# Layer 1's second table made inside the rounds, and the order of the lagging block and of the last groups

## The chip, the cores and the metric

The kernel runs on one core of one Trainium2 chip. A core has five engines with an instruction queue each: TensorE (PE) multiplies matrices into PSUM, VectorE (DVE) and ScalarE (ACT) compute on SBUF and PSUM, GpSimd (POOL) here mostly issues gathers, and SyncE (SP) issues plain transfers. Each engine takes its instructions strictly in order and waits on semaphores where an instruction needs the result of another engine or of a transfer. The metric is the time of one execution on the device, in microseconds (us); the verdict compares medians over several runs.

## The reference

A graph network of two layers over 6250 nodes with 128 features and 106250 edges sorted by their target `dst`. Cut to what matters:

```python
h = relu(layernorm(x))
# layer 0: attention over the edges of each target
xl, xr = h @ Wl + bl, h @ Wr + br
m = leaky_relu(xl[src] + xr[dst] + edge_weight1 @ We, 0.2)
logits = m @ att
ex = exp(logits - segment_max(logits, dst)[dst])
out = segment_sum(xl[src] * ex, dst) / (segment_sum(ex, dst) + 1e-16) + bias_out
h = gelu(h + out)
x = x + batchnorm(h)                 # mean and variance over all nodes
# layer 1: messages
h = relu(layernorm(x))
em = concat([h[src], h[dst]]) @ msg_w + msg_b
em = relu(layernorm(em) * msg_g + msg_beta) * edge_weight
messages = segment_sum(em, dst) / count
gate = sigmoid(h @ gate_w + gate_b)
h_new = relu(layernorm(concat([h, messages]) @ upd_w + upd_b) * upd_g + upd_beta)
x = x + gate * h_new + (1 - gate) * h
```

## The kernel before

**Two arms.** A flag is computed on the chip from `dst`. Where the targets are sorted and every block of 1024 edges touches few enough nodes, the arm `fast()` runs, else `general()`. The conditions are columns of the tile `wide`, four before the change (L282 to L292).

**Tables.** Layer 0 gathers rows of `xl_d` by `src`. Layer 1 uses linearity: `h[src] @ msg_w[:128]` and `h[dst] @ msg_w[128:]` are computed per node into the tables `a_d` (the source ends) and `b_d` (the target ends, "the other ends"). `a_d` is gathered by `src`, so all of it must be written before the first gather. `b_d` is read in windows of 126 consecutive rows, because the targets of one block are consecutive.

**Rounds.** Both layers walk 104 blocks (`NS`) of 1024 edges (8 tiles of 128), one block `s` per round: eight gathers on POOL (`gather`, L200), a window of the target table into `W` (`load`, L878), a product with a one-hot matrix that spreads the window over the edges (`spread`, `expand` L895), DVE and ACT work, and a product with a second one-hot matrix `oh` that sums a block's edges into its window (`agg_ps`, L1110 and L1370). The sums go to `res0_d` or `res1_d` (`flush`, `store` L898).

**The lagging block.** In layer 0 the sums need the maximum of each target, which is found for four blocks at a time (`maxima`, a generator of eight working steps that alternate between DVE and PE). So round `s` also finishes block `u = s - 7`: its one-hot `oh` (L1079), its weights `glw` (L1082, and eight scalings at L1094 on ACT; after the last gather half of them at L1092 on DVE), its product (L1110). After the last gather, eight rounds (`s` = 104 to 111) work off the lag. In layer 1 the lag is one block.

**Groups of nodes.** A group of four node tiles is finished (`nodes` in layer 0, `nodes1` in layer 1, also generators) once every block that can touch it has been stored; `rounds_of` gives the round. The last group (13 groups, the last of two tiles) can only start after the last block: `both` alternates its steps with those of the group before.

**The middle.** Between the layers lie the batch norm (`bn`, L1150 to L1158) and a loop over 13 chunks of 512 nodes: `mix` (DVE), `centre` (PE), `split` (ACT and POOL), a product `var_ps` for the variance, and one product `mm` per tile of 128 nodes (L1203), 257 columns wide: 128 for `a_d`, 128 for `b_d`, one for the gate. ACT scales the `b_d` half and the gate (L1212), DVE the `a_d` half (L1213), SP writes both (L1216, L1217).

**Order.** Inside `tc.manual_schedule()` the order on each engine is that of the program text; semaphores are placed automatically. A tile of a pool with one buffer can be filled again only when all readers of the one before are done. The PSUM pool `ps_1` of layer 1 has one buffer for each of the tags `nt`, `nz`, `agg1_ps` and the constants.

Of the kernel before, what the change touches and what calls it, by code (L numbers as in the profile page):

```python
# [16 lines left out]
P = 128  # L17
# [23 lines left out]
SLACK = 96  # L41
TN = 4
# [11 lines left out]
def kernel(  # L54
# [167 lines left out]
    with tc.tile_pool(name="pre", bufs=2) as pp, tc.tile_pool(name="pre1", bufs=1) as p1, tc.tile_pool(  # L222
# [59 lines left out]
        wide = p1.tile([NS, 4], F32, name="wide")  # L282
# [8 lines left out]
        for k in range(4):  # L291
            V.tensor_add(nbad[:NS, :], nbad[:NS, :], wide[:, k : k + 1])  # L292
# [452 lines left out]
    def fast():  # L745
# [165 lines left out]
        def both(a, b):  # L911

            left = [b, a]
            while left:
                for g in list(left):
                    if next(g, True):
                        left.remove(g)
# [9 lines left out]
        with tc.tile_pool(name="e0", bufs=2) as ep, tc.tile_pool(  # L927
# [61 lines left out]
            def nodes(g):  # L989
# [36 lines left out]
                S.activation(hT_sb[:, ns], hT_sb[:, ns], AF.Gelu)  # L1026
                yield
# [21 lines left out]
            steps, group = None, None  # L1049
# [9 lines left out]
            for s in range(NS + LAG + 1):  # L1059
# [10 lines left out]
                if s < NS:  # L1070
                    ps = pss.pop(s)
                    V.tensor_tensor(ps, ps, gl[:, :, :D], ALU.add)  # L1072
                    S.activation(ps, ps, AF.Relu)  # L1073
                if steps is not None:
                    next(steps, None)
                if 0 <= u < NS:
                    b, q = divmod(u, SB)
                    oh = ep.tile([P, ST, P], F32, name="oh")
                    V.tensor_tensor(oh, over_tiles(iota_ps, ST), over_features(dl_c[:, u, :], ST),  # L1079
                                    ALU.is_equal)  # L1080
                    glw = ep.tile([P, ST, W0], F32, name="glw")
                    V.tensor_copy(glw[:, :, D:], exm[b][:, q])  # L1082
                if s + 2 < NS:
                    one_hot_t(ps_1, "mx", s + 2, 0, *wins[s + 2])
                if u >= 1 and s < NS:
                    flush(u - 1)
                if 0 <= u < NS:
                    glu = gls.pop(u)
                    for j in range(ST):
                        f = exm[b][:, q, j, 1:2]  # L1090
                        if s >= NS and j % 2:
                            V.tensor_scalar(glw[:, j, :D], glu[:, j, :D], f, None, op0=ALU.mult)  # L1092
                        else:
                            S.activation(glw[:, j, :D], glu[:, j, :D], AF.Copy, scale=f)  # L1094
                if s >= NS:
                    flush(u - 1)
                if s < NS:
# [13 lines left out]
                if s < NS and s % SB == SB - 1:  # L1111
                    steps = maxima(s // SB)
                    next(steps, None)
                elif steps is not None:
                    next(steps, None)
# [14 lines left out]
            both(group, nodes(NGR - 1))  # L1130
# [9 lines left out]
        wm = fs.tile([P, 2 * D + 1], F32, name="wm")  # L1140
        V.tensor_copy(wm[:, : 2 * D], w1[:, : 2 * D])
        V.tensor_copy(wm[:, 2 * D :], w1[:, 3 * D : NW1])
        with tc.tile_pool(name="md", bufs=2) as mp, tc.tile_pool(
# [44 lines left out]
            for c in range(NC):  # L1188
# [11 lines left out]
                for j in range(n):  # L1200
                    t = c * TN + j
                    mm = ps_t.tile([P, 2 * D + 1], F32, name="mm")
                    T.matmul(mm, hT_sb[:, t * P : (t + 1) * P], wm, start=True, stop=True)  # L1203
                    outs.append(mm)
# [4 lines left out]
                tab = mp.tile([P, TN, 2 * D + 1], F32, name="tab")  # L1209
                for j, mm in enumerate(outs):  # L1210
                    r = rstd_c[:, c * TN + j : c * TN + j + 1]
                    S.activation(tab[:, j, D:], mm[:, D:], AF.Copy, scale=r)  # L1212
                    V.scalar_tensor_tensor(tab[:, j, :D], mm[:, :D], r, b1[:, :D], op0=ALU.mult, op1=ALU.add)  # L1213
                V.tensor_copy(gate[:, ts], tab[:, :n, 2 * D])
                rows_ = slice(c * CH, c * CH + n * P)
                nc.sync.dma_start(a_d[rows_].rearrange("(t p) f -> p t f", p=P), tab[:, :n, :D])  # L1216
                nc.sync.dma_start(b_d[rows_].rearrange("(t p) f -> p t f", p=P), tab[:, :n, D : 2 * D])  # L1217
# [7 lines left out]
        with tc.tile_pool(name="e1g", bufs=6) as gp, tc.tile_pool(name="e1", bufs=2) as ep, tc.tile_pool(  # L1225
# [22 lines left out]
            def nodes1(g):  # L1248
# [7 lines left out]
                yield  # L1256
# [11 lines left out]
                yield  # L1268
                mT = e1.tile([P, m, P], F32, name="mT", tag="mT" + z_)
                z = e1.tile([P, m, D], F32, name="z", tag="z" + z_)  # L1270
                tp = ps_1.tile([P, TN, P], F32, name="nt")
                for j in range(n):
                    T.transpose(tp[:, j, :], fin[:, 0, j, :D], ident)
                S.copy(mT[:, :n, :], tp[:, :n, :])
                yield
                zp = ps_1.tile([P, TN, D], F32, name="nz")
                for j in range(n):
                    T.matmul(zp[:, j, :], mT[:, j, :], u2, start=True, stop=False)
                    T.matmul(zp[:, j, :], h_sb[:, t0 + j, :], w1[:, 2 * D : 3 * D], start=False, stop=True)
                for j in range(n):  # L1280
                    V.scalar_tensor_tensor(z[:, j, :], zp[:, j, :], rstd_c[:, t0 + j : t0 + j + 1],
                                           b1[:, 2 * D : 3 * D], op0=ALU.mult, op1=ALU.add)
                yield
# [19 lines left out]
                tp = ps_1.tile([P, TN, P], F32, name="nt")  # L1303
                xp = ps_1.tile([P, TN, P], F32, name="nz")
                for j in range(n):
                    T.transpose(tp[:, j, :], h_sb[:, t0 + j, :], ident)
                    T.transpose(xp[:, j, :], x_sb[:, t0 + j, :], ident)
                for j in range(n):
                    V.scalar_tensor_tensor(z[:, j, :], tp[:, j, :], keep[:, t0 + j : t0 + j + 1], z[:, j, :],
                                           op0=ALU.mult, op1=ALU.add)  # L1310
# [7 lines left out]
            group = None  # L1318
            due = rounds_of(1)
            for s in range(2):  # L1320
# [5 lines left out]
            for s in range(NS + 2):  # L1326
                u = s - 1
                if s + 2 < NS:
# [42 lines left out]
                if s in due:  # L1371
                    finish(group)
                    group = nodes1(due[s])
                if group is not None:
                    next(group, None)
            both(group, nodes1(NGR - 1))
# [49 lines left out]
```

## Time and profile before

| | us |
|---|---|
| three runs | 2317.82, 2320.14, 2320.94 (median 2320.14) |
| the profiled execution, its time | 2316.21 |
| its span (first to last instruction) | 2314.1 |
| first gather of layer 0 starts | 61.2 |
| last gather of layer 0 issued | 1104.4 |
| first gather of layer 1 starts | 1216.7 |
| last gather of layer 1 issued | 2256.4 |

Busy time over the span, of the page's first part: POOL 1611.4 us (70%), DVE 1766.5 (76%), PE 1437.2 (62%), ACT 1273.6 (55%). A line of the timeline gives the start, the duration, the engine, the source line, the operation, the tiles, and in square brackets how long the engine had been idle before and what ended the idle time. A line of the windows view gives the stretch, its length, the busy time and the number of instructions of PE, weight loads, DVE, ACT and POOL, then the granted clock of PE, the share of the DMA engines and GB/s.

### The profile page before, as it was taken

The page shows a single profiled execution, that of the slowest core. Times are in us where ns is not written, and L with a number is a line of the kernel's source. Part 1 is how long each engine was busy: PE and PEld are TensorE (multiplying, and loading weights), DVE is VectorE, ACT ScalarE, POOL GpSimd, SP SyncE. Part 2 cuts the span into 40 slices and gives each one's busy share as a digit, 9 for nine tenths or more (in the row PEclk, how much of TensorE's full clock was granted, in tenths as well). Part 3 has the DMA queues.
Part 4 walks back from the last instruction along what each step waited for, and adds up shares of the span by engine and source line. Part 5 has one row for each costly group of instructions (what it writes and reads, how often), then busy time and mean ns, then how long its engine had stood idle before and what let it go on. Part 6 is the DMA issues. An engine that isn't in the chain of part 4 may idle for free.

```text
span 2314.1 us, 30585 instructions
## 1 busy us (share of the span) xinstructions
PE 1437.2 (62%) x8206; PEld 1245.6 (54%) x8206; DVE 1766.5 (76%) x3795; ACT 1273.6 (55%) x4208; POOL 1611.4 (70%) x1703
## 2 busy tenths in 40 slices
PE   5656666566656666666585666666665666566663
PEld 4545555455555555556464555555555555555553
DVE  5578788788788788777655777797797887788786
ACT  5224344443344344443465776777777777777674
POOL 1777777777777777777037777777777777777770
PEclk9679878887787878887787777888888788888886
DMA  5742343332332332332132222232233233233231
GB/s 149 179 132 68 87 142 107 76 76 67 76 77 67 76 77 67 77 76 66 40 112 61 67 76 75 70 80 78 68 80 80 64 80 81 66 81 79 67 79 28
DMA packets 187647, 188.13 MB, mean 81 GB/s; under 512 B 38256, under 2 KB 154960, under 8 KB 187464
## 3 DMA queue, kind: packets, MB, share of 16 engines
q0 software_dynamic: 53792, 110.57, 19.8%
q1 hardware_dynamic: 130812, 75.25, 11.3%
q8 instruction: 66, 1.08, 0.2%
q10 hardware_dynamic: 2860, 0.27, 0.1%
q14 instruction: 117, 0.96, 0.1%
HBM read 142.91 MB, written 43.04 MB: 80 GB/s over the span
## 4 chain that ended last, share of the span: by engine, by line
POOL 31%; DVE 25%; issue 14%; DMA 12%; PE 10%; ACT 6%; DVEq 0%; POOLq 0%; ACTq 0%; another core or an unknown queue 0%; SPq 0%
POOL gl L200 31%; DMA gl<-xl_d,src_c 8%; DVE y L1354 4%; DMA gl<-a_d,src_c 3%; PE agg_ps L1370 3%; DVE m_ps L1072 3%; DVE y L1338 2%; DVE oh L1349 2%; DVE y L1356 2%; ACT sq L1343 2%; DVE oht L891 2%; ACT y L1357 1%; ACT glw L1360 1%; PE mm L1203 1%; DVE lr L1100 1%
## 5 line engine op out<-in xcount | busy, mean ns | idle before, releaser
L200 POOL DMA_INDIRECT gl<-xl_d,src_c x832 | 790.6, 950 | 298.8 <-issue 230.4
L200 POOL DMA_INDIRECT gl<-a_d,src_c x832 | 787.4, 946 | 261.0 <-issue 226.2
L1370 PEld LDWEIGHTS agg_ps<-glw,oh 128*128 128x128 f32 x1664 | 314.3, 272 | 481.6 <-ACT glw L1360 481.6
L890 PE MATMUL dlp<-dl_b,ident_b 104*128 104x512 bf16 x416 | 179.3, 431 | 607.4 <-DVE oht L891 500.1
L1110 PEld LDWEIGHTS agg_ps<-glw,oh 128*128 128x128 f32 x1664 | 295.8, 267 | 228.6 <-ACT glw L1094 209.8
L1370 PE MATMUL agg_ps<-glw,oh 128*128 128x129 f32 x1664 | 341.1, 382 | 90.7 <-ACT glw L1360 81.3
L891 DVE TENSOR_SCALAR oht<-dlp,iota_p 126x512 f32<-126x512 f32 x416 | 309.7, 744 | 97.9 <-PE dlp L890 97.9
L1343 ACT ACTIVATE sq<-y 128x128 f32<-128x128 f32 x832 | 256.9, 309 | 225.3 <-DVE y L1338 202.4
L1073 ACT ACTIVATE m_ps<-m_ps 128x1024 f32<-128x1024 f32 x104 | 104.9, 1008 | 501.1 <-DVE m_ps L1072 249.3
L1110 PE MATMUL agg_ps<-glw,oh 128*128 128x130 f32 x1664 | 299.1, 355 | 22.6 <-ACT glw L1094 10.5
L895 PE MATMUL m_ps<-W,oht 128*128 128x128 f32 x1664 | 255.5, 317 | 12.1 <-DMA oht<-in_edge_weight_dram 6.2
L1072 DVE TENSOR_TENSOR m_ps<-m_ps,gl 128x1024 f32<-128x1024 f32 x104 | 128.0, 1231 | 173.6 <-DMA gl<-xl_d,src_c 164.5
L1360 ACT ACTIVATE glw<-y,ew_c 128x128 f32<-128x128 f32 x832 | 254.5, 389 | 3.4
L895 PEld LDWEIGHTS m_ps<-W,oht 128*128 128x128 f32 x1664 | 238.5, 229 | 20.8 <-DVE lr L1100 11.0
L1094 ACT ACTIVATE glw<-gl,exm 128x128 f32<-128x128 f32 x804 | 245.9, 393 | 0.1
L895 PEld LDWEIGHTS y_ps<-W,oht 128*128 128x128 f32 x1664 | 223.4, 216 | 8.9 <-issue 7.2
L895 PE MATMUL y_ps<-W,oht 128*128 128x128 f32 x1664 | 227.0, 295 | 0.0
L1354 DVE SCALAR_TENSOR_TENSOR y<-y,rs,cst 128x128 f32<-128x128 f32 x832 | 223.2, 340 | 0.0
L1338 DVE TENSOR_TENSOR y<-y_ps,gl 128x1024 f32<-128x1024 f32 x104 | 125.3, 1205 | 47.4 <-DMA gl<-a_d,src_c 45.7
L1343 ACT ACTIVATION_READ_ACCUMULATOR sq<-y 128x1 f32 x832 | 155.0, 186 | 0.0
L1357 ACT ACTIVATE y<-y 128x1024 f32<-128x1024 f32 x104 | 109.9, 1056 | 44.2 <-DVE y L1356 44.2
L1100 DVE TENSOR_REDUCE lr<-m_ps 128x8 f32<-128x1024 f32 x104 | 127.3, 1224 | 3.6
(255 smaller groups left out, 1769.2 us busy)
## 6 DMA issues: line engine op xcount, KB each, us to landing
gl<-xl_d,src_c POOLq DMA_INDIRECT x832
gl<-a_d,src_c POOLq DMA_INDIRECT x832
res<-agg SPq DMA_DIRECT2D x104, 64.0 KB
res<-agg SPq DMA_DIRECT2D x104, 63.5 KB
W<-xr_d SPq DMA_DIRECT2D x104, 63.0 KB
W<-b_d SPq DMA_DIRECT2D x104, 63.0 KB
res<-zt SPq DMA_DIRECT2D x20, 325.0 KB
res<-zt SPq DMA_DIRECT2D x20, 322.5 KB
```

What stands on the lines that cost most here:

```text
L200: GP.indirect_dma_start(out=dest, out_offset=None, in_=table, in_offset=bass.IndirectOffsetOnAxis(ap=idx, axis=0))
L890: T.matmul(dlp, ident_b[:NS, s : s + 1].to_broadcast([NS, P]), dl_b[:, es], start=True, stop=True)
L891: V.tensor_scalar(oht[:WIN, es], dlp[:WIN, :], iota_p[:WIN, :], None, op0=ALU.is_equal)
L895: T.matmul(ps[:, j, :], oht[:, j * P : (j + 1) * P], w, start=True, stop=True)
L1072: V.tensor_tensor(ps, ps, gl[:, :, :D], ALU.add)
L1094: S.activation(glw[:, j, :D], glu[:, j, :D], AF.Copy, scale=f)
L1110: T.matmul(aggs[u], oh[:, j, :], glw[:, j, :], start=(j == 0), stop=(j == ST - 1))
L1338: V.tensor_tensor(y, pss.pop(s), gl, ALU.add)
L1343: S.activation(sq, y[:, j, :], AF.Square, accum_out=rs[:, j : j + 1])
L1354: V.scalar_tensor_tensor(yu[:, j, :], yu[:, j, :], ru[:, j : j + 1], mg_ps, op0=ALU.mult, op1=ALU.mult)
L1360: S.activation(glw[:, j, :D], yu[:, j, :], AF.Copy, scale=ew_c[:, u, j : j + 1])
L1370: T.matmul(aggs[u], oh[:, j, :], glw[:, j, :], start=(j == 0), stop=(j == ST - 1))
```

## The change

1. A fifth column of `wide`: a block whose first target lies beyond 61 times its number plus 64 sets the flag.
2. In layer 0's round the order of the lagging block changes: `oh`, `glw`, the scalings and the store of block `u` come ahead of the work on block `s`, and a step of `maxima` comes after them (except in every fourth round, where it stays right behind `oh`).
3. `both` becomes `in_turn`: the steps of the last two groups follow a written order. In layer 0's last group one `Sqrt` of a constant is added behind the `Gelu`.
4. In the middle the product shrinks to 129 columns, DVE scales all of it in one instruction per tile, ACT no longer scales anything and takes the copy of the gate column from DVE. The `b_d` rows of the first 512 nodes are made there, behind chunk 1.
5. The other twelve pieces of `b_d` are made in rounds 1, 9, 18, 26, 34, 43, 51, 60, 68, 76, 85 and 93 of layer 1: four products at the end of the round into the PSUM tile `nt`, one DVE multiplication and one transfer at the start of the next.
6. `nodes1` is cut into other steps: all its PSUM tiles share the tag `nz`, a wait of one round behind `fetch` goes, products and their readers lie in different rounds. In the last rounds the group before the last is only fetched in round 103, and the one before that is finished in round 104.

```diff
+LEAD = 61
+AHEAD = 64
...
+        V.tensor_scalar(wide[:, 4:5], iota_p[:NS, :], float(LEAD), float(AHEAD), op0=ALU.mult, op1=ALU.add)
+        V.tensor_tensor(wide[:, 4:5], dst_r[:, 0:1], wide[:, 4:5], ALU.is_gt)
-        for k in range(4):
+        for k in range(5):
...
-        def both(a, b):
-            left = [b, a]
-            while left:
-                for g in list(left):
-                    if next(g, True):
-                        left.remove(g)
+        def in_turn(a, b, order):
+            for c in order:
+                next(a if c == "a" else b, None)
+            finish(a)
+            finish(b)
...
                 S.activation(hT_sb[:, ns], hT_sb[:, ns], AF.Gelu)
+                if last:
+                    S.activation(std_c[:, 0:1], eps, AF.Sqrt)
...
-                if s < NS:
-                    ps = pss.pop(s)
-                    V.tensor_tensor(ps, ps, gl[:, :, :D], ALU.add)
-                    S.activation(ps, ps, AF.Relu)
-                if steps is not None:
-                    next(steps, None)
                 if 0 <= u < NS:
                     b, q = divmod(u, SB)
                     oh = ep.tile([P, ST, P], F32, name="oh")
...
+                    if q == 0:
+                        next(steps, None)
                     glw = ep.tile([P, ST, W0], F32, name="glw")
                     V.tensor_copy(glw[:, :, D:], exm[b][:, q])
-                if s + 2 < NS:
-                    one_hot_t(ps_1, "mx", s + 2, 0, *wins[s + 2])
-                if u >= 1 and s < NS:
-                    flush(u - 1)
-                if 0 <= u < NS:
                     glu = gls.pop(u)
...
-                if s >= NS:
+                if u >= 1:
                     flush(u - 1)
+                if s < NS:
+                    ps = pss.pop(s)
+                    V.tensor_tensor(ps, ps, gl[:, :, :D], ALU.add)
+                    S.activation(ps, ps, AF.Relu)
+                if u < 0 or u % SB:
+                    next(steps, None)
+                if s + 2 < NS:
+                    one_hot_t(ps_1, "mx", s + 2, 0, *wins[s + 2])
...
-            both(group, nodes(NGR - 1))
+            in_turn(group, nodes(NGR - 1), "baabbbabbab")
...
-        wm = fs.tile([P, 2 * D + 1], F32, name="wm")
+        wm = fs.tile([P, D + 1], F32, name="wm")
+        def b_product(ps, g):
+            n = min(TN, NT - g * TN)
+            for j in range(n):
+                t = g * TN + j
+                T.matmul(ps[:, j, :], hT_sb[:, t * P : (t + 1) * P], w1[:, D : 2 * D], start=True, stop=True)
+        def b_rows(pool, ps, g):
+            t0, n = g * TN, min(TN, NT - g * TN)
+            tab = pool.tile([P, TN, D], F32, name="tab_b")
+            V.tensor_tensor(tab[:, :n, :], ps[:, :n, :], over_features(rstd_c[:, t0 : t0 + n], n), ALU.mult)
+            nc.sync.dma_start(b_d[t0 * P : (t0 + n) * P].rearrange("(t p) f -> p t f", p=P), tab[:, :n, :])
...
-                    S.activation(tab[:, j, D:], mm[:, D:], AF.Copy, scale=r)
-                    V.scalar_tensor_tensor(tab[:, j, :D], mm[:, :D], r, b1[:, :D], op0=ALU.mult, op1=ALU.add)
-                V.tensor_copy(gate[:, ts], tab[:, :n, 2 * D])
+                    V.scalar_tensor_tensor(tab[:, j, :], mm, r, b1[:, : D + 1], op0=ALU.mult, op1=ALU.add)
+                S.copy(gate[:, ts], tab[:, :n, D])
...
-                nc.sync.dma_start(b_d[rows_].rearrange("(t p) f -> p t f", p=P), tab[:, :n, D : 2 * D])
+                if c == 1:
+                    bp = ps_t.tile([P, TN, D], F32, name="b_ps", tag="mm")
+                    b_product(bp, 0)
+                    b_rows(mp, bp, 0)
...
                 fetch(fin, res1_d, t0, n)
                 yield
-                yield
...
-                yield
...
-                tp = ps_1.tile([P, TN, P], F32, name="nt")
+                tp = ps_1.tile([P, TN, P], F32, name="nt", tag="nz")
                 for j in range(n):
                     T.transpose(tp[:, j, :], fin[:, 0, j, :D], ident)
+                yield
                 S.copy(mT[:, :n, :], tp[:, :n, :])
-                yield
                 zp = ps_1.tile([P, TN, D], F32, name="nz")
...
+                yield
                 for j in range(n):
...
-                yield
                 mv = small.tile([P, TN, 2], F32, name="mv1")
...
-                tp = ps_1.tile([P, TN, P], F32, name="nt")
-                xp = ps_1.tile([P, TN, P], F32, name="nz")
-                for j in range(n):
-                    T.transpose(tp[:, j, :], h_sb[:, t0 + j, :], ident)
+                hp = ps_1.tile([P, TN, P], F32, name="nh", tag="nz")
+                for j in range(n):
+                    T.transpose(hp[:, j, :], h_sb[:, t0 + j, :], ident)
+                yield
+                for j in range(n):
+                    V.scalar_tensor_tensor(z[:, j, :], hp[:, j, :], keep[:, t0 + j : t0 + j + 1], z[:, j, :],
+                                           op0=ALU.mult, op1=ALU.add)
+                xp = ps_1.tile([P, TN, P], F32, name="nx", tag="nz")
+                for j in range(n):
                     T.transpose(xp[:, j, :], x_sb[:, t0 + j, :], ident)
-                for j in range(n):
-                    V.scalar_tensor_tensor(z[:, j, :], tp[:, j, :], keep[:, t0 + j : t0 + j + 1], z[:, j, :],
-                                           op0=ALU.mult, op1=ALU.add)
+                yield
                 V.tensor_tensor(z[:, :n, :], z[:, :n, :], xp[:, :n, :], ALU.add)
...
+            early = {(CH * g - AHEAD - WIN + 1 - 2 * LEAD) // LEAD - 2: g for g in range(1, NCH)}
...
+                if made is not None:
+                    b_rows(ep, *made)
+                    made = None
...
+                if s in early:
+                    made = ps_1.tile([P, TN, D], F32, name="b_ps1", tag="nt"), early[s]
+                    b_product(*made)
-                if s in due:
+                if s in due and s < NS - 1:
                     finish(group)
                     group = nodes1(due[s])
-                if group is not None:
+                if group is not None and s < NS - 1:
                     next(group, None)
-            both(group, nodes1(NGR - 1))
+                if s == NS - 1:
+                    late, last = nodes1(due[s]), nodes1(NGR - 1)
+                    next(late)
+                if s == NS:
+                    finish(group)
+                    next(late)
+            in_turn(late, last, "baaababababa")
```

## The prediction

> **What bounds the kernel now.** I read first the list of costliest groups:
>
> ```profile
> L200 POOL DMA_INDIRECT gl<-xl_d,src_c x832 | 790.6, 950 | 298.8 <-issue 230.4
> L200 POOL DMA_INDIRECT gl<-a_d,src_c x832 | 787.4, 946 | 261.0 <-issue 226.2
> ```
>
> A gather takes 0.94 us and the next starts 0.30 later: 832 at 1.248 are 1038.3 us. Layer 0 took 1044.1 (61.2 to 1105.3), layer 1 1040.7 (1216.7 to 2257.4). In the rounds nothing but POOL counts; a block takes 8 x 1.248 = 9.98 us there. The gaps without gathers remain: 61.2 us in front, 111.4 between the layers, 56.7 at the end. Next, the windows of two pieces of the middle gap:
>
> ```profile
> 1105.00:1160.00 55.00, 26.80 (x147) 23.30 (x146) 35.31 (x116) 22.80 (x60) 0.33 (x1) 0.75 0.16 35
> 1174.00:1210.00 36.00, 36.00 (x194) 29.50 (x193) 20.79 (x71) 27.52 (x74) 19.88 (x11) 1.00 0.49 148
> ```
>
> In the drain of layer 0 no engine is full (DVE 35 of 55): it waits in a ring. In the chunks of the middle PE is busy all 36 us. Then the timeline, the drain:
>
> ```profile
> 1120.46 0.21 DVE L956 TENSOR_TENSOR_SCAN srow<-kS,tx 1x32 f32<-1x32 bf16 x1 [2.21 <-PE tx L952]
> 1126.10 0.15 DVE L969 COPY cc<-tx 32x2 f32<-32x2 f32 x1 [3.11 <-PE tx L966]
> 1133.23 0.19 DVE L982 TENSOR_TENSOR exm<-tx,fst_c 128x32 f32<-128x32 f32 x1 [2.79 <-PE tx L978]
> 1145.71 2.06 PE L1110 MATMUL agg_ps<-glw,oh 128*128 128x130 f32 x16 [0.40 <-ACT agg L1046]
> 1160.07 1.28 ACT L1151 ACT_TABLE_LOAD   x1 [1.05 <-DVE bmv L1150]
> ```
>
> DVE waits for a `maxima` transpose queued on PE behind `agg_ps`, and the next block's `oh` is behind that wait. One chunk of the middle, and the end:
>
> ```profile
> 1181.15 0.69 ACT L1179 ACTIVATE sq<-ctr,bn 128x512 f32<-128x512 f32 x1 [0.55 <-PE ctr L1173]
> 1181.70 1.98 PE L1203 MATMUL mm<-wm,h_sb 128*128 128x257 f32 x8
> 1182.31 0.26 ACT L1207 ACTIVATE std_c<-var_ps,eps 128x4 f32<-128x4 f32 x1
> 1182.60 0.18 DVE L1208 RECIPROCAL rstd_c<-std_c 128x4 f32<-128x4 f32 x1 [0.89 <-ACT std_c L1207]
> ...
> 2257.00 1.13 DVE L1281 SCALAR_TENSOR_TENSOR z<-nz,rstd_c,b 128x128 f32<-128x128 f32 x4 [7.01 <-PE nz L1279]
> 2276.40 0.69 DVE L1298 TENSOR_TENSOR z<-z,ug_r 128x512 f32<-128x512 f32 x1 [4.78 <-ACT z L1295]
> 2290.06 0.27 ACT L1245 COPY agg<-agg_ps 128x129 f32<-128x129 f32 x1 [1.49 <-PE agg_ps L1370]
> 2294.88 0.16 DVE L1258 TENSOR_TENSOR inv<-fin 128x2 f32<-128x2 f32 x1 [1.44 <-DMA fin<-res]
> ```
>
> At the end DVE waits 7.01 and 4.78 us for steps of `nodes1` that stand in front of the last blocks' work.
>
> **Layer 0's drain (1113.6 to 1147.8).** DVE's waits for transposes are 1.59 (L943), 2.21, 3.11 and 2.79: 9.7 us. After the change `oh` (pitch 1.13), `glw` (0.15) and four scalings (0.86), 2.1 us in all, stand ahead of each step, so PE multiplies while DVE prepares the next block; PE needs 2.0 to 3.8 us a block (L1110) plus 0.2 to 0.4 for transposes, DVE 2.1 plus the step's 0.75 to 1.6. I leave 1.6 us of waits, and the last block's logits come 0.2 earlier (no `oh` between): 8.3 gained, `agg_ps` of block 103 ending at 1139.5. Bounds: 5 (half the waits stay, PE at the slow 3.8) and 9.9.
>
> **Layer 0's last groups (1147.8 to 1161.65).** Both `Exp` now come before both `Gelu`, and the `Sqrt` table loads under the statistics. From the end of the last store's copy (1139.8): store and fetch 4.5 (as 2290.33 to 2294.88), maxima 0.75, the other group's `h_sb` 0.65, scaling 2.0, transposes 0.5, `h_sb` 0.5, `Gelu` 0.45, statistics 1.0, rest of the table load and the root 0.85: 1151.0 against 1161.65, so 2.4 gained beyond the drain (bounds 1 and 4). The rows price a table switch at 1.28 us and the next activation at 1.30 after it. The Trainium skill, "ScalarE: Activation LUTs", section "What ACT_TABLE_LOAD costs", adds a drain of about 1.38 us to each; no row here shows it. By the page two removed switches would save some 2.8 us more.
>
> **The middle.** PE per chunk now: `ctr` 0.86, `var_ps` 0.79, `mm` 1.84, sum 3.49, the period. With 129 columns the nearest row is 128 columns at 0.117 per instruction (`m_ps` L895, 16 in 1.87): 8 are 0.94, sum 2.59. But ACT's copy of the gate waits for DVE's last scaling, and the next chunk's `sq` is queued behind it on ACT. Ring: `sq` 0.58, `h_sb` 0.57, root 0.29, reciprocal 0.21, four scalings from PSUM 1.13 (L1281, four), hand-over 0.05, copy 0.1 (as L984 to L1046): 2.95. So this ring takes PE's place. Ten periods: (3.49 - 2.95) x 10 = 5.4, the last being 2.84 now, less 0.6. `b_ps` behind chunk 1 waits for a `mm` buffer and pushes `ctr` of chunk 3: -0.9. In chunk 0 PE is slow (3.77 for `mm`), half of it goes, 2.0 of it seen by `sq` of chunk 2. Behind the last `sq`: 3.55 to the last `a_d` write instead of 4.47: 0.9. Total 6.8. The removed 13 ACT groups of scalings and `b_d` writes lie inside this. SP's loads of `W` now wait for the first `b_d` piece in front of an `a_d` write; SP needs 0.36 a chunk, covered, up to 2 us for one chunk otherwise. Bounds: ring at 3.35 (copy and hand-overs at the 0.26 of L1207 and 0.2): 2.8; PE alone (2.59): 10. A rule against it: the Trainium skill, "VectorE: DVE Perf Modes", section "The TRN2 errata", gives SBUF sources a fixed 224 cycles on ScalarE but 58 on VectorE. By it a copy of four elements is an estimated 0.19 us on ACT, the ring 3.04, and the gain 0.9 less; rows of 0.14 to 0.16 (DVE, L1214) and 0.19 (ACT, L984) agree on the ACT side.
>
> **`b_d` in the rounds.** Twelve times 0.94 on PE, 0.74 on DVE (512 wide, as L1168), a write and SP's next `W` load behind it, about 5 us, needed a round later. DVE stands at the round's start for a product queued behind `agg_ps`: that ended 2.2 us after the next `y` began (1710.80, 1713.00), so 3.2 + 0.7 = 3.9 us late, and `y`, `sq` and all behind them with it. Cover: a round of layer 1 needs 7.53 us (`y` at 1703.27, 1710.80) against 9.98, 20.6 us over 8.4 rounds; a group takes 9.5 of DVE, and its waits of 7.0 and 1.4 go by the new cuts. 14.4 of 20.6, with six gather buffers behind. Cost 0; without the cover 12 x 3.9 = 47.
>
> **The end.** `y` of block 103 ran at 2265.6, its gather landed at 2259.8. With the 7.01 gone and no group work in round 103, it runs at 2260.0. Round 103: 5.6 of DVE, then ACT `y` and `glw` 3.5, `agg_ps` to 2270.6; the copy, block 103's `y`, `glw` and product take 5.2 more: 2275.8 against 2290.03. Some is given back: DVE's last sum of group 10 waits for transposes behind that product (2277.5), and its output write stands on SP ahead of the last store, so store and fetch land at 2282.8, not 2280.5. Group 11 scales from 2277.5 to 2280.2, transposes and copy to 2281.2, product 2283.3, scaling and statistics 2285.5, `z` 2287.6. Group 12 scales 2286.3 to 2288.5; then both share the one buffer `nz`: copy 2289.2, transposes 2290.5, group 11's use 2291.2, group 12's product 2293.1, statistics 2294.7, `z` 2297.0, three weights 2298.4, use 2299.0, transposes 2300.0, sum 2300.5. Before: 2309.84. Gain 9.3; bounds 3.5 (`y` 103 as late as before) and 11.
>
> **The rest at nothing.** The fifth condition's DVE work, 0.12 + 0.15 + 0.13 (L289, L290, L292), lies under DVE's idle 1.0 to 1.5 per `tl` group; 0.4 without. On these inputs every block's first target is at least 61 rows inside the new bound. Layer 0's rounds: the relu on ACT stands behind eight `glw` (2.44), which no longer wait for the gather and are done before it lands.
>
> **Sum.** 8.3 + 2.4 + 6.8 + 9.3 = 26.8: span 2287.3, execution 2316.21 - 26.8 = 2289.4. The median shown was 3.9 above that execution, so 2293.3; I say 2294.
>
> **Rivals.** *Half of it* (chance 0.14): the middle's ring at 3.35 and the end chained by `nz` and a late `y`: 6 + 1 + 2.8 + 3.5 = 13, time 2307. For it: one buffer, one SP queue; against: the 14 us by which block 103 moves. *Slower* (0.05): in layer 0, if DVE reaches a round late, the eight `glw` run after the landing and the relu waits all of 2.44 with DVE idle. DVE is busy 808.7 of 1045, 7.78 a round; with 2.44, the relu's 1.01, less 0.65 of `oht` it is 10.58 against 9.98: 104 x 0.6 = 62, time 2356. It decides from 10.24 a round (26.8/104). Against it: 2.2 us of slack and three rounds of gather buffers. *It doesn't do what it says* (0.03): the freed waits are taken up by PE or the clock, within 4 us of 2320. Forecast: 0.78.
>
> **Numbers.** The range of the likeliest is 2286 (gains 9.9, 4, 10, 11 not all at once) to 2304; to leave no more than 2 in 10 out I take 2286 to 2309. About 0.2%, 4.6 us, can be told from no change. Faster: 0.91, same 0.04, slower 0.05.
>
> **What would show it.** First gather of layer 1 at 1199 (1216.7 - 17.5); `agg_ps` of block 103 in layer 0 ending near 1139.5; `sq` in the middle every 2.95 us with PE no longer full; both gather groups' busy time and the 1044 and 1040 us unchanged; 47 us from the last gather's end to the end of the span. Wrong if a gather's idle time is ended by DVE or ACT for more than a few us, or if the middle keeps 3.4.

## The result and the profile after

The changed kernel takes 2297.57 us (median of four runs, 2292.04 to 2299.08) against 2320.54 (four runs); the ratio is 0.9884, 95% interval 0.9856 to 0.9912. The forecast was 2294, range 2286 to 2309. The profiled execution took 2297.45 with a span of 2295.6, so 18.5 less than the span of before; 26.8 were forecast. Cut at the gathers, the two spans are:

| stretch (us) | before | after | gained | forecast |
|---|---|---|---|---|
| front: start to first gather of layer 0 | 61.23 | 68.52 | -7.3 | 0 |
| gathers of layer 0 | 1044.1 | 1044.2 | 0 | 0 |
| last gather to the copy of block 103's sums | 42.5 | 33.9 | 8.7 | 8.3 |
| from there to the root of the variance | 13.8 | 11.3 | 2.5 | 2.4 |
| from there to the first gather of layer 1 | 55.0 | 46.8 | 8.2 | 6.8 |
| gathers of layer 1 | 1040.7 | 1041.6 | -0.9 | 0 |
| last gather to the end of the span | 56.7 | 49.3 | 7.4 | 9.3 |

The list of costliest groups of the changed kernel shows that the gathers cost what they did (busy, mean ns, idle before):

```profile
L202 POOL DMA_INDIRECT gl<-xl_d,src_c x832 | 791.0, 951 | 305.1 <-issue 224.6
L202 POOL DMA_INDIRECT gl<-a_d,src_c x832 | 788.3, 948 | 261.3 <-issue 237.7
```

The windows of the drain and of part of the middle (length, then busy PE, weight loads, DVE, ACT, POOL, granted clock):

```profile
1112.50:1158.00 45.50, 26.13 (x144) 22.93 (x144) 33.97 (x114) 21.08 (x57) 0.17 (x1) 0.69 0.20 42
1171.00:1195.00 24.00, 23.73 (x157) 18.99 (x156) 16.18 (x50) 12.05 (x31) 13.84 (x9) 1.00 0.34 106
```

DVE is busy 34.0 of 45.5 us in the drain; before it was 35.3 of 55. The work is nearly the same; DVE's idle time in the drain fell from 19.7 us to 11.5. Two lines of the timeline before the change, the copy of block 103's sums and the root of the variance, at which the middle gap is cut in the table:

```profile
1147.85 0.27 ACT L1046 COPY agg<-agg_ps 128x130 f32<-128x130 f32 x1 [2.19 <-PE agg_ps L1110]
1161.36 0.29 ACT L1151 ACTIVATE bn<-bmv,eps 128x1 f32<-128x1 f32 x1
```

The timeline of the changed kernel, with the waits that were shown of before (L956, L969, L982 and the table load are now L959, L972, L985 and L1031), that copy and that root:

```profile
1126.53 0.21 DVE L959 TENSOR_TENSOR_SCAN srow<-kS,tx 1x32 f32<-1x32 bf16 x1 [0.40 <-PE tx L955]
1128.98 0.14 DVE L972 COPY cc<-tx 32x2 f32<-32x2 f32 x1
1132.37 0.18 DVE L985 TENSOR_TENSOR exm<-tx,fst_c 128x32 f32<-128x32 f32 x1
1146.54 0.27 ACT L1051 COPY agg<-agg_ps 128x130 f32<-128x130 f32 x1 [2.19 <-PE agg_ps L1114]
1156.17 1.28 ACT L1031 ACT_TABLE_LOAD   x1
1157.58 0.28 ACT L1167 ACTIVATE bn<-bmv,eps 128x1 f32<-128x1 f32 x1
```

Waits of 2.21, 3.11 and 2.79 have become 0.40 and none. In the middle, one chunk to the next:

```profile
1183.14 0.20 ACT L1229 COPY gate<-tab 128x4 f32<-128x4 f32 x1 [1.46 <-DVE tab L1228]
1183.24 0.68 ACT L1195 ACTIVATE sq<-ctr,bn 128x512 f32<-128x512 f32 x1
1184.96 1.13 DVE L1228 SCALAR_TENSOR_TENSOR tab<-mm,rstd_c,b 128x129 f32<-128x129 f32 x4
1186.12 0.20 ACT L1229 COPY gate<-tab 128x4 f32<-128x4 f32 x1 [1.46 <-DVE tab L1228]
1186.22 0.68 ACT L1195 ACTIVATE sq<-ctr,bn 128x512 f32<-128x512 f32 x1
```

From `sq` to `sq` are 2.98 us (3.49 before), and ACT stands 1.46 of them at the gate copy, waiting for DVE: the ring of the forecast (2.95). The copy lasts 0.20, but the next `sq` starts 0.10 after the copy does, as the forecast had it. At the end:

```profile
2250.25 1.23 DVE L1362 TENSOR_TENSOR y<-y_ps,gl 128x1024 f32<-128x1024 f32 x1 [3.17 <-PE nh L1321]
2257.49 3.81 PE L1394 MATMUL agg_ps<-glw,oh 128*128 128x129 f32 x16 [7.12 <-ACT glw L1384]
2263.05 3.81 PE L1394 MATMUL agg_ps<-glw,oh 128*128 128x129 f32 x16 [1.75 <-ACT glw L1384]
2267.39 0.69 DVE L1330 TENSOR_TENSOR z<-z,nx 128x512 f32<-128x512 f32 x1 [5.91 <-PE nx L1328]
2274.91 0.87 DVE L1298 SCALAR_TENSOR_TENSOR z<-nz,rstd_c,b 128x128 f32<-128x128 f32 x3 [4.07 <-PE nz L1295]
```

`y` of block 103 now runs 4.0 us after the last gather (8.2 before). It needs the product `y_ps`, which ended at 2243.9, and the eight gathers; the `nh` that the line names is no input of it (in `g_tail`, below, `y` ran 0.6 us ahead of that `nh`). But DVE then waits 5.9 us for transposes queued behind the product of block 103, and 4.1 for a product.

**The front.** The 7.3 us lost there lie in code that is the same but for the fifth condition. The window 40 to 60 us of four traces, in this order: before, after, a second trace of the kernel before (`before_again`), and `g_tail` (below), which holds the fifth condition too:

```profile
40.00:60.00 20.00, 12.69 (x78) 9.54 (x77) 7.02 (x26) 12.22 (x31) 0.00 (x0) 0.93 0.35 102
```

```profile
40.00:60.00 20.00, 17.25 (x66) 12.95 (x66) 7.64 (x38) 12.77 (x34) 0.00 (x0) 0.53 0.28 82
```

```profile
40.00:60.00 20.00, 17.38 (x65) 13.11 (x65) 6.83 (x32) 12.09 (x31) 0.00 (x0) 0.51 0.27 81
```

```profile
40.00:60.00 20.00, 12.83 (x78) 9.66 (x78) 7.07 (x28) 11.73 (x30) 0.00 (x0) 0.94 0.34 97
```

The first gather came at 61.2, 68.5, 68.9 and 60.6: late wherever PE's granted clock had fallen to half by then, with the old kernel as with the new. Over 14 traces the two kinds were seven each (60.6 to 62.8; 67.4 to 71.1); in two of the late ones the recorded clock stays at 1.00 while PE's products are as slow as in the other five. So two traces can differ by 7 us with no change in the kernel; compared without the front, the change gained 25.8 of the 26.8 forecast.

### The profile page after: what moved, and what is told of

The parts are those of the page before. It is cut to its first block, busy times and chain, and to the rows that moved or that the text cites. A ratio compares the mean times of both kernels' runs of the same rounds, so it can differ in the third digit from the quotient of the medians.

```text
span 2295.6 us, 30619 instructions
## 1 busy us (share of the span) xinstructions
PE 1437.9 (63%) x8304; PEld 1245.5 (54%) x8304; DVE 1775.9 (77%) x3798; ACT 1265.5 (55%) x4171; POOL 1609.8 (70%) x1703
## 4 chain that ended last, share of the span: by engine, by line
POOL 36%; DVE 24%; issue 17%; DMA 13%; PE 7%; ACT 3%; DVEq 0%; ACTq 0%; another core or an unknown queue 0%; POOLq 0%; SPq 0%
POOL gl L202 36%; DMA gl<-xl_d,src_c 7%; DMA gl<-a_d,src_c 4%; DVE m_ps L1095 3%; DVE y L1378 3%; DVE oht L895 3%; DVE y L1362 2%; PE agg_ps L1394 2%; DVE y L1380 2%; DVE oh L1373 2%; DVE lr L1104 1%; DVE m_ps L1102 1%; DVE oh L1078 1%; PE m_ps L899 1%; DMA dst_r<-in_dst_dram 1%
## 5 line engine op out<-in xcount | busy, mean ns | idle before, releaser
L895 DVE TENSOR_SCALAR oht<-dlp,iota_p 126x512 f32<-126x512 f32 x416 | 309.6, 744 | 105.3 <-PE dlp L894 104.9
L1114 PEld LDWEIGHTS agg_ps<-glw,oh 128*128 128x128 f32 x1664 | 290.8, 263 | 171.9 <-ACT agg L1051 52.4
L1114 PE MATMUL agg_ps<-glw,oh 128*128 128x130 f32 x1664 | 293.7, 350 | 10.5 <-ACT agg L1051 6.8
L1102 DVE TENSOR_TENSOR m_ps<-m_ps,att 128x1024 f32<-128x1024 f32 x104 | 127.0, 1221 | 16.3 <-ACT m_ps L1096 15.9
```

Source lines behind the costliest of these rows:

```text
L895: V.tensor_scalar(oht[:WIN, es], dlp[:WIN, :], iota_p[:WIN, :], None, op0=ALU.is_equal)
L1114: T.matmul(aggs[u], oh[:, j, :], glw[:, j, :], start=(j == 0), stop=(j == ST - 1))
```

## The experiments

Two of the runs fell on a chip on which the kernel before took 2320.11 (median of nine). The other ten fell where it took 3254, 3242 and 3272 (medians of three sessions; the record numbers their chips 8 for `a` to `d`, 10 for `e`, `i`, `j` and `k`, and 0 for `l` and `before_again`; that of the first two runs is 6). There the gathers take the same 0.95 us each, but the rounds are late: in stretches of some 12 us ACT and PE start their instructions 1.4 to 2.1 us apart. ACT's squares, 0.43 apart elsewhere, in the timeline of `d_gate_dve`:

```profile
2322.64 0.31 ACT L1367 ACTIVATE sq<-y 128x128 f32<-128x128 f32 x1 [1.73 <-remote]
2324.76 0.31 ACT L1367 ACTIVATE sq<-y 128x128 f32<-128x128 f32 x1 [1.72 <-remote]
2326.85 0.30 ACT L1368 ACTIVATE rs<-rs,eps 128x8 f32<-128x8 f32 x1 [1.69 <-remote]
```

What causes these is not known. Below "chip 1" is the first and "chip 2" stands for the others; on chip 2 the stretch from the copy of block 103's sums to the first gather of layer 1 can still be read (68.8 and 68.9 us in the two traces of the kernel before), while the drain (51.4 against 42.5) and the times there answer another question: what the change does when the rounds have no time over.

| run | chip | time, ratio to before (95%) | layer 0 | layer 1 | behind it |
|---|---|---|---|---|---|
| `a2_drain_old` | 1 | 2302.91, 0.9915 (0.9891 to 0.9940) | 1043.3 | 1041.1 | 49.1 |
| `g_tail` | 1 | 2277.85, 0.9825 (0.9805 to 0.9844) | 1044.9 | 1040.8 | 41.0 |
| `before_again` | 2 | 3282.06, one run | 1488.6 | 1497.2 | 104.9 |
| `a_drain_old` | 2 | 3220.73, 0.9884 (0.9845 to 0.9924) | 1471.5 | 1473.1 | 98.7 |
| `b_ends_old` | 2 | 3265.62, 1.0030 (1.0001 to 1.0059) | 1547.1 | 1465.6 | 97.0 |
| `c_b_middle` | 2 | 3257.95, 1.0009 (0.9978 to 1.0041) | 1520.8 | 1460.6 | 99.1 |
| `d_gate_dve` | 2 | 3265.74, 1.0044 (1.0014 to 1.0073) | 1521.3 | 1475.2 | 97.4 |
| `e_nodes1_old` | 2 | 3318.95, 1.0213 (1.0145 to 1.0280) | 1519.2 | 1521.5 | 104.2 |
| `i_warm` | 2 | 3248.60, 1.0008 (0.9967 to 1.0048) | 1518.4 | 1470.3 | 90.6 |
| `j_new_late` | 2 | 3309.52, one run | 1551.5 | 1474.0 | 98.7 |
| `k_old_late` | 2 | 3253.91, one run | 1496.1 | 1474.3 | 97.4 |
| `l_relu_first` | 2 | 3282.98, 1.0052 (1.0010 to 1.0093) | 1560.5 | 1475.3 | 91.5 |

Here "layer 0" and "layer 1" are the stretches of their gathers.

### The drain (`a_drain_old`, `a2_drain_old`)

Layer 0's round as before the change, all else changed; both runs are the same kernel.

```diff
+                if s < NS:
+                    ps = pss.pop(s)
+                    V.tensor_tensor(ps, ps, gl[:, :, :D], ALU.add)
+                    S.activation(ps, ps, AF.Relu)
+                if steps is not None:
+                    next(steps, None)
                 if 0 <= u < NS:
                     b, q = divmod(u, SB)
                     oh = ep.tile([P, ST, P], F32, name="oh")
...
-                if u < 0 or u % SB:
-                    next(steps, None)
```

> The changed kernel with layer 0's round order of before (part 2 undone, all else kept). In the changed kernel's trace agg of block 103 is copied 33.8 us after the last gather of layer 0 ends, before the change 42.5. Theory (DVE waited for transposes behind the products, and the new order fills those waits): the copy comes back to 42.5, the gap without gathers between the layers goes from 92.0 to 100.7, the time from 2297.6 to 2306. Rival (the drain is set by PE's products at a reduced clock, the order moves little): gap 92 to 95, time 2298 to 2301. Both expect the gathers of layer 0 to take 1044 as in both kernels; if the new order costs or saves anything in the rounds, this number moves.

> The same kernel as a_drain_old (layer 0's round order of before, all else changed), since that one ran on a chip on which the rounds themselves were late. Theory: where the gathers set the rounds, agg of block 103 is copied 42.5 us after the last gather of layer 0 (33.9 in the changed kernel), the gap is 100.7, the gathers of layer 0 take 1044 in either order, the time is 2306. Rival (the drain is set by PE at a reduced clock): gap 92 to 95, time 2298 to 2301. Where the rounds are late again as on that chip: layer 0's gathers some 50 us shorter than those of the changed order, since the relu no longer stands behind eight scalings on ACT.

On chip 1 the copy of block 103's sums came 43.9 us behind the last gather (42.5 expected, 33.9 with the new order), and layer 0's gathers took the same 1043 to 1044: the order is worth 10.0 us in the drain and nothing in the rounds. The gap was 104.0, not 100.7. Besides the drain, the third `sq` of the middle came 2.1 us later behind the second (5.07 against 3.00): in the timeline of `a2_drain_old` the eight `mm` products of chunk 0 and those of chunk 1 take

```profile
1174.12 2.07 PE L1222 MATMUL mm<-wm,h_sb 128*128 128x129 f32 x8
1178.41 1.14 PE L1222 MATMUL mm<-wm,h_sb 128*128 128x129 f32 x8
```

at a granted clock of 0.50 and then 1.00; in the changed kernel both took 1.14. On chip 2 the old order was quicker in the rounds by 49 to 76 us than the new one in `b`, `c` and `d` (one trace each).

### The last groups of layer 0 (`b_ends_old`)

```diff
-            in_turn(group, nodes(NGR - 1), "baabbbabbab")
+            both(group, nodes(NGR - 1))
...
-                if last:
-                    S.activation(std_c[:, 0:1], eps, AF.Sqrt)
```

> The changed kernel with the last two groups of layer 0 in strict alternation again and without the early Sqrt (part 3 undone). Theory: from the copy of block 103's sums to the root of the variance 13.8 us instead of 11.4 (before the change 13.9), gap 92.0 + 2.4 = 94.4, time 2300. Rival (the two removed table loads lay beside the fetch and cost nothing): 11.4 to 12, gap 92 to 92.6, time 2298. By the Trainium skill, page ScalarE: Activation LUTs, section What ACT_TABLE_LOAD costs, a switch costs 2.66 with its drain, and two of them an estimated 5.3: gap 97.3.

From the copy to the root: 14.0 us, against 11.1 to 11.5 in `c`, `d`, `e`, `i` and `j`, all on chip 2. The theory holds (13.8 against 11.4). The two more table loads took 1.28 each; where the next activation had its input, it began 0.01 later. The 5.3 us by the page are not seen. What the order gives alone, and what the early `Sqrt`, was not separated.

### The middle (`c_b_middle`, `d_gate_dve`)

`c` has products 257 wide and all of `b_d` in the middle again; `d` is one line:

```diff
-                S.copy(gate[:, ts], tab[:, :n, D])
+                V.tensor_copy(gate[:, ts], tab[:, :n, D])
```

> The changed kernel with all of b_d made in the middle again, products 257 wide and ACT scaling half of them (parts 4 and 5 undone). Theory: a chunk takes 3.49 again (2.98 now), gap 92.0 + 8.2 = 100.2, time 2306; layer 1's gathers take 1041 as now, since the pieces in the rounds cost nothing that the gathers see; the lag of y behind the last gather of its block, at most 5.9 now, gets smaller in the rounds that follow a piece. Rival (the pieces in the rounds cost the gathers or the end something): layer 1's gathers or the 49.3 us behind them get shorter by that, and the time ends below 2306.

> The changed kernel with the copy of the gate column on DVE as before the change (one line). Theory (the ring sq, h_sb, root, reciprocal, four scalings, copy, next sq sets the period of 2.98, and PE needs 2.65): the period falls to 2.65, ten periods give 3.3, gap 88.7, time 2294.3. Rival (another wait, such as the PSUM buffers of mm or DVE itself, takes its place at once): period 2.9 to 3.0, gap 91 to 92, time 2297 to 2298.

The periods were 3.49 and 2.65, both as expected to 0.01. So PE sets the period before the change, the ring through ACT's gate copy does after it, and without that copy it is PE again. From the first `sq` to the first gather `d` needed 38.4 us, the changed kernel 42.3: 3.9 less, where the ten periods were to give 3.3.

But `c` did not bring back the 8.2 us expected of it. Over the same stretch it needed 47.7, so 5.4 more than the changed kernel; before the change it was 50.5. The difference is chunk 0. Its eight `mm` products in the timelines of before, of `c` and of the changed kernel:

```profile
1169.20 3.77 PE L1203 MATMUL mm<-wm,h_sb 128*128 128x257 f32 x8
1656.64 1.98 PE L1218 MATMUL mm<-wm,h_sb 128*128 128x257 f32 x8
1164.88 1.14 PE L1219 MATMUL mm<-wm,h_sb 128*128 128x129 f32 x8
```

Before the change they ran at a granted clock of 0.50, in `c`, as wide, at 1.00. The clock goes with layer 0's order: in the five traces with the old order (`before`, `before_again`, `a`, `a2`, `k`) these products ran at 0.50, in the nine others at 1.00. From the second `sq` to the third it took 6.31 us before the change, 5.07 with the narrow product and the old order (`a2`), 3.55 with the wide product and the new order (`c`), and 3.00 with both. So 2.1 to 2.8 of the 3.3 us came with part 2 of the change, and 0.6 to 1.2 with the narrower product. For the rounds see `e`.

### The end (`g_tail`)

The gate copy on DVE, and a new order at the end. Its core:

```diff
+                if s == NS - 1:
+                    ahead()
+                if s == NS:
+                    next(group)
+                    flush1(u - 1)
...
+                if s == NS:
+                    next(late)
+                    next(late)
+                    next(group)
+                    mixed(NGR - 2)
+                    mixed(NGR - 1)
+            bring(NGR - 1)
+            finish(group)
+            in_turn(late, last, "aabbaabbbababbba")
```

`ahead` makes the transposes of x for groups 10 to 12 and of h for groups 11 and 12 in the free `y_ps` buffers, `mixed` their sum with the gate's weight, `bring` fetches the last group, and the two generators are cut finer.

> The changed kernel with the gate column copied by DVE and the end of layer 1 written out anew: the transposes of h and x for the last groups stand in PE's idle time ahead of the products of block 102, the next to last group is scaled in DVE's idle time while block 103 is multiplied, the sums of block 102 are copied by DVE, the last store goes ahead of the output of group 10, and the transposes of the means have their own PSUM buffer. Theory (at the end the engines wait for steps queued in a poor order, as the changed kernel's 5.9 and 4.1 us of DVE waits there say): the stretch from the last gather to the end of the span falls from 49.3 to about 40; the gap between the layers from 92.0 to 88.1; the time from 2297.6 to about 2284. Rival (the end is bound by PE at half its clock and by the store and fetch of the last block, so the order moves little): 45 to 49 behind the last gather, time 2290 to 2294.

Behind the last gather 41.0 us (40 expected), gap 87.8 (88.1), time 2277.85. That is 6 us below the 2284 expected; the profiled execution (2276.95) had a front of 60.6 us, that of the changed kernel 68.5, and the fronts of the others are not known. The timeline of `g_tail` shows how: the last sums of block 102 copied by DVE, the next to last group scaled at once, the last group as soon as it has landed, and its `z` and last sum:

```profile
2249.29 0.28 DVE L1264 COPY agg<-agg_ps 128x129 f32<-128x129 f32 x1
2249.48 0.15 DVE L1294 TENSOR_TENSOR inv<-fin 128x3 f32<-128x3 f32 x1
2257.22 0.16 DVE L1294 TENSOR_TENSOR inv<-fin 128x2 f32<-128x2 f32 x1 [1.17 <-DMA fin<-res]
2265.13 0.61 DVE L1318 SCALAR_TENSOR_TENSOR z<-nz,rstd_c,b 128x128 f32<-128x128 f32 x2 [3.72 <-PE nz L1315]
2269.80 0.89 DVE L1342 TENSOR_TENSOR z<-z,hx 128x256 f32<-128x256 f32 x2
```

Counted from the last gather's end (2234.2) group 11 is scaled at 15.3 instead of 21.7 and group 12 at 23.0 instead of 31.4. This version beats both kernels on chip 1.

### PE's clock (`i_warm`)

`g_tail` with products that nobody reads in PE's idle time.

```diff
+        def warm(pool, tag, n):
+            t = pool.tile([P, P], F32, name="warm", tag=tag)
+            for _ in range(n):
+                T.matmul(t, ident, ident, start=True, stop=True)
```

> g_tail with matrix products whose result nobody reads added in stretches in which PE is idle: 12 behind the last product of layer 0, 10 and 14 between the transposes of its last groups and the small product of the batch norm, 3 behind that, and 16 ahead of the product of block 102 in layer 1. In g_tail the granted clock of PE falls to 0.5 there, the first four ctr products take 3.78 us (2.04 for four at full clock) and the two last agg products 3.67 and 2.54. Theory (the granted clock follows what PE did in the microseconds before): the ctr products take about 2.0, the gap falls from 87.8 to about 85.5, the product of block 102 takes 2.0 to 2.5, the stretch behind the last gather 41.0 to about 40, the time 2278 to about 2274. Rival (the clock is taken back for a time whatever PE does, or for having been busy): the products keep 3.7, gap and end as in g_tail or longer, time 2278 to 2281.

In the timeline of `i_warm`, the added products and the first four `ctr` products (3.78 in `g_tail`):

```profile
1649.47 2.84 PE L919 MATMUL warm<-ident 128*128 128x128 f32 x24
1654.50 1.98 PE L1202 MATMUL ctr<-x_sb,cen 128*128 128x512 f32 x4
```

From the copy of the last sums to the first gather 52.4 us; 54.1 in `d_gate_dve`, also on chip 2, 54.3 in `g_tail`. The granted clock was 1.00 from 1643 to 1658 us; in the same stretch of `g_tail` (1144 to 1156) it was 0.50. So here the clock follows what PE did just before, and 1.7 to 1.9 us hang on it. In layer 1 the product of block 102 took 2.53 behind the added products (3.67 in `g_tail`); the stretch to the end can't be compared, since the run was on chip 2; its time on chip 1 was not measured.

### The pieces of `b_d` in the rounds (`e_nodes1_old`)

`nodes1` and the end as before the change, the pieces still in the rounds. The last lines of its edit:

```diff
...
-            in_turn(late, last, "baaababababa")
+            both(group, nodes1(NGR - 1))
```

> The changed kernel with nodes1 and the end of layer 1 as before the change (part 6 undone), while the twelve pieces of b_d stay in the rounds. Before the change y lagged up to 12.6 us behind the last gather of its block and rose slowly all through layer 1, so the old cuts left no time over. Theory (the pieces are hidden only because the new cuts give the DVE waits of 7.0 and 1.4 us back): each piece adds up to 3.9 us of lag, the lag of y grows to 30 to 50 us by the end of layer 1, the gathers still take 1041 or a little more, the stretch behind the last gather grows from 49.3 to 75 to 100, the time is 2325 to 2350. Rival (a piece costs DVE its 0.74 us only, and the cuts matter for the end alone): lag 8 to 15, 57 to 62 behind the last gather, time 2305 to 2310.

On chip 2 layer 1's gathers took 1521.5; with the new cuts 1465.6 to 1475.3; with the new cuts and no pieces (`c`) 1460.6; with the old cuts and no pieces (`before_again`) 1497.2. So where no time is over twelve pieces cost 24 us under the old cuts (2.0 each) and 5 to 15 under the new ones, and the cuts themselves give 37 back. These are differences of single traces from different sessions; the seven traces with the new cuts and the pieces lie 10 us apart. Behind the last gather `e` needed 104.2, like the kernel before (104.9), against 97.0 to 99.1 with the changed kernel's end (`a` to `d`, `j`, `k`): the new end gives 5 to 7 us there too. The times of the expectation do not apply on this chip; of its two prices for a piece, 3.9 and 0.74, neither is right here, and what a piece costs under the old cuts on chip 1 was not measured.

### The slower rival (`j_new_late`, `k_old_late`, `l_relu_first`)

`j` and `k` make `oh` three times in the new and the old order of layer 0; `l` is `i_warm` with the relu put ahead of the scalings:

```diff
+                if s < NS:
+                    ps = pss.pop(s)
+                    V.tensor_tensor(ps, ps, gl[:, :, :D], ALU.add)
+                    S.activation(ps, ps, AF.Relu)
                 if 0 <= u < NS:
                     b, q = divmod(u, SB)
...
```

> The changed kernel with the one-hot oh of the lagging block computed three times in each of layer 0's rounds (the same values), 2.26 us more DVE work in each of 97 rounds, so that the rounds are late by DVE on this chip too. Theory (the slower rival of the prediction is real: where a round is late the relu on ACT waits behind eight glw of 2.44 us while DVE waits for the relu): layer 0's gathers take at least 30 us longer here than in k_old_late, some 1150 to 1250. Rival (the order makes no difference, and what the first chip showed came from its slow transfers): within 10 us of k_old_late.

> The same two extra oh in a2_drain_old, so with layer 0's round order of before. DVE busy 7.78 + 2.26 = 10.04 us a round and some waits on top. Theory: layer 0's gathers take 1080 to 1180, at least 30 us less than in j_new_late, since the relu stands ahead of the scalings on ACT. Rival: within 10 us of j_new_late.

> i_warm with the sum and the relu of block s put back ahead of the lagging block's work in layer 0's rounds (the order of before for these two instructions alone). On a chip on which the gathers set the rounds: layer 0's gathers 1044 as ever, gap about 86 (87.8 in g_tail, less the 1.9 that the idle-time products gave between the copy of the last sums and the first gather), the stretch behind the last gather 40 to 41, time about 2275. On the chip on which the rounds were late: Theory (the relu behind eight glw is what cost the new order some 50 us there): layer 0's gathers 1465 to 1500 instead of 1518, time some 20 to 50 us below i_warm's 3249. Rival (another part of the old order did it, such as the steps of maxima or the one-hots): layer 0's gathers 1510 to 1530, time as i_warm.

> The kernel before, unchanged, for a second trace of it. Theory (the 7.3 us by which the changed kernel's first gather came later are not its doing: PE's granted clock falls to 0.5 in some executions at 40 us and in others at 55): the first gather starts at 60 to 63 or at 68 to 70, and which of the two goes with the clock granted between 40 and 60 us (0.93 or more, or 0.5). On the chip with late rounds: layer 0's gathers 1465 to 1500 (the old order), layer 1's 1470 to 1490, so that e_nodes1_old's 1521 is 30 to 50 us more than before, which is the price of the twelve pieces where the old cuts give them no time.

`j` and `k` fell on chip 2, where they can't tell the theories apart: the difference of 55 us is that of the orders there anyway. `l` decides: with the relu first, layer 0 took 1560.5, no less than the 1518 of `i_warm`, and 72 more than `before_again`, whose chip bears the same number. The theory of the relu falls. `before_again` itself had the front expected of it (68.9 us at a clock of 0.51) and the layer 0 (1488.6); its layer 1 took 1497.2 where 1470 to 1490 were expected, so the price of the pieces in `e` is 24 and not 30 to 50. On chip 2 layer 0's gathers took 1471 to 1496 in the old order (three traces, `k` with its added work) and 1518 to 1561 in the others (seven, `j` with its added work); which part of the new order costs these 22 to 89 us stays open.

## Why the prediction was right, point by point

- **Gathers set the rounds, and nothing there changes:** right on chip 1 (1044 and 1041 us in every trace).
- **The drain, 8.3:** 8.7. The waits named fell from 9.7 in all to 0.4 on the shown lines; undoing the order alone brought back 10.0. That the order would also bring chunk 0 of the middle back to full clock was not foreseen.
- **The last groups, 2.4:** 2.5, and 2.5 to 2.8 in the undoing.
- **The middle, 6.8:** 8.2. The ring through the gate copy was the right bound (2.95 forecast, though its terms add up to 2.93; 2.98 measured; 2.65 without it). Three sizes were off: the periods gave 8 x 0.51 - 0.5 = 3.6 where 4.8 were forecast; chunk 0 gave 3.3 where 2.0 were; behind the last `sq` 2.1 where 0.9 were (8.3 us before the change and in `c`, 6.2 after; SP no longer writes `b_d` between the last rows and the first gather). `b_ps` cost 0.8 (0.9 forecast). In chunk 0 the reason failed too: the forecast put its gain down to the narrower product, which gives 0.6 to 1.2; the rest is the clock, by the drain's order. So the sum of the middle came near partly by luck.
- **`b_d` in the rounds, 0:** 0.9 lost in layer 1's gathers. `y` lags at most 5.9 us behind its block's last gather, 12.6 before the change, so the cover is there; of the 0.9, 0.5 is the last gather's own length (1.46 instead of 0.94), and two more traces of chip 1 with the pieces took 1041.1 and 1040.8. The two terms named for what the cover had to bear, 9.5 and 3.9, add up to 13.4, where 14.4 is said. The price without it (47) is not tested on chip 1; on chip 2 it was 24.
- **The end, 9.3:** 7.4. The order was as forecast; `y` of block 103 came 1.3 later behind the last gather than forecast, and the two last products took 3.81 each at a granted clock of 0.5 (3.49 and 3.45 before the change). Block 103's product ended 20.6 us behind the last gather where 18.5 were forecast, and the rest kept that delay. The last gather took 1.46 here instead of 0.94, but that is not why `y` was late: in `a2_drain_old` and `g_tail`, with last gathers of 1.05 and 0.94, `y` came 4.0 and 3.9 behind them. Why is open.
- **The rest at nothing:** right as to the change, but the term "the sum is made against that execution" failed: its front was of the short kind, that of the profiled execution after of the long kind, 7.3 us apart. The 3.9 us added for the median covered half of it.
- **The sum:** the parts missed by 0.4, 0.1, 1.4, -0.9 and -1.9 us and came to 25.8 where 26.8 were forecast; that the total is so near is in part luck.
- **Rivals:** half of it fell (middle and end gave 15.6 of the 16.1 forecast for them). The slower one did not occur on chip 1; on chip 2 the new order of layer 0 does cost some tens of microseconds, but not through the relu.

## What to carry to other kernels

Cut two traces at the same events (first and last gather) before a difference of totals is explained; here a front that flips by 7 us hid that the parts came out within 2 us each. When a bound engine is relieved, look for the ring that is next: a copy of four elements on the wrong queue held the period at 2.98 where PE needed 2.65. An order that is free while another engine sets the pace is not free everywhere: on chip 2 the variants that kept the new order of layer 0 were no quicker than the kernel before (ratios 1.001 to 1.021). And a new order in one stage can change PE's clock in the next: undo parts one at a time before a gain is put down to one of them.

## What the runs showed of the hardware

In the changed kernel's trace the granted clock of PE fell from 1.00 to 0.5 at 41 us, though from 33 to 60 us PE never paused for more than 0.6; four more traces show the same fall. In the middle it stayed at 1.00 with added work, where it was 0.50 without. The Trainium skill, "TensorE: Matmul & The Clock Gate", section "Part 1: The HAM clock gate (the "warmup" mystery)", has the clock rise after about 3.4 us of sustained work and fall after an idle stretch as long: `i_warm` agrees (with PE's idle time filled, the clock did not fall), the front does not. In two traces (`b`, `l`) the clock's row says 1.00 there while 66 matmuls took 17.3 us as at half clock, so the products' durations are the better witness. And in three sessions, on chips that the record numbers 8, 10 and 0, the same program took 40% longer, with gathers of the same 0.95 us.
